# A GNN attention layer: leaky scores by absolute values, softmax sums once per chunk, and in the last chunk three of seven weight tiles made by ScalarE

## The chip, the cores and the metric

One core of one Trainium2 chip runs the whole program. The metric is the device time of one execution in microseconds (us); the kernel before took 5410.82 us (median of three runs, 5407.89 to 5411.46). The engines are TensorE (PE, with its weight loads as PEld), VectorE (DVE), ScalarE (ACT), GpSimd (POOL) and the DMA queues, most of which SyncE (SP) issues. Each engine works its own queue in order; they wait for one another by semaphores.

## The reference

A pre-norm graph attention layer on 12,500 nodes of 128 features and 412,500 edges of 64 features, cut to what matters:

```python
h = relu(layernorm(x))
q, k, v = h @ Wq + bq, h @ Wk + bk, h @ Wv + bv
attn_in = concatenate([q[src], k[tgt], edge @ We + be])
hmid   = leaky_relu(attn_in @ A1 + b1, 0.2)          # per edge, 128
scores = leaky_relu(hmid @ A2 + b2, 0.2)             # per edge, 8 heads
w      = softmax(scores.mean(heads), over all edges)
out    = segment_sum(w * v[tgt], src)
x + gamma * norm(h @ Wn + bn + out) + beta
```

A leaky value is linear in z and |z|: leaky(z) = 0.6 z + 0.4 |z| for a slope of 0.2. So the mean over eight heads is a sum of eight absolute values and one linear form, sum(z).

## The kernel before, in words

**Staging.** The edges are cut into four chunks (121, 109, 98 and 75 groups of 1024 edges). The first stage computes, for each tile of 128 edges, the k part of the hidden row and v (L809, L812), evicts them with ScalarE (L792, L795) and scatters each row by an indirect DMA of GpSimd (`scatter`, L747) into a table in HBM that is sorted into 98 blocks of 128 source nodes. The second stage reads each block back as 11, 10, 9 or 7 tiles of 128 slots (chunks 0 to 3) and does the rest. The first stage of chunk c+1 runs interleaved with the second stage of chunk c. The second stage of chunk 3, "the last chunk" below, has no first stage beside it. Then a final stage norms the nodes (L1193 to L1204).

**A block in the second stage**, with its jobs in `second_stage`: `load` brings the rows from HBM to `rows_of` (SP, L834; six buffers) and q for the block (L837). `places` turns the place column on PE (L841), `put_places` writes it out by ACT and a DMA (L846, L848), `spread_places` reads it back to all partitions (SP, L854), and `select` compares it on DVE (L861, `sel_q`). `turn` transposes four or three tiles on PE and adds q through `sel_q` (L870, L873) into `h_ps`; `steep` is the hidden leaky value, ACT (L881, `low`) and then DVE (L882). `heads_of` multiplies with A2 on PE (L889) into the one bank `s_ps`; `add_bias` evicts it with ACT (L896, `z`); `by_slot` is the scores' leaky value and a 32x32 transpose on DVE (L902, L904); `scores` masks and sums the heads on DVE (L910, L912, L916). `spread_top` transposes the row maxima on PE (L921), `greatest` keeps the running maximum on DVE (L930), `exponentials` makes exp and a fading factor on ACT (L938 or L941, L943), and `add_weights` adds to the sums on DVE (L948). `weights` makes one 128x128 matrix for each tile on DVE (L955: place equal to column, times the weight), `products` multiplies it with v on PE (L964, two passes for each tile), and `add_sums` adds the block into `acc` on DVE (L971, L973).

**What sets the order.** A plan written out by hand: `at(step, turn, job, block)` puts each job at a step, a step's jobs go by their turn, and each engine takes its instructions in exactly that order. A block of the last chunk has two quads (`nq` = 2; four tiles, then three) and takes four steps, so its plan repeats every four steps, with jobs of several blocks in each. `load` of a block may be issued when the products of the block six before it have been read.

The plan's repeating order before, in the last chunk, for one period:

```
PE:  places | products x3 | turn x3 | spread_top | products x4 | heads_of | turn x4
DVE: add_sums | weights x4 | greatest | steep x3 | select | weights x3 | add_weights | leaky | transpose | none | summed | score | steep x4
ACT: put_places | steep x3 | exp, fade | add_bias | steep x4
```

Of the kernel before, what the change touches and what calls it, by code (L numbers as in the profile page):

```python
# [10 lines left out]
FP = mybir.dt.float32  # L11
# [4 lines left out]
AF = mybir.ActivationFunctionType  # L16
ALU = mybir.AluOpType
AX = mybir.AxisListType
# [4 lines left out]
P = 128  # L23
D = 128
DE = 64
H = 8
EPS = 1e-5
SLOPE = 0.2
# [8 lines left out]
BUFS = 6  # L37

RROWS = 16

SPARE = 2

# [69 lines left out]
def kernel(ctx: ExitStack, tc: tile.TileContext, n_edges, x, src, dst, ea, w_nv, w_qt, w_kt,  # L112
# [12 lines left out]
    nc = tc.nc  # L125
    NP = x.shape[0]
    NTN = NP // P
# [8 lines left out]
    for i, share in enumerate(CHUNKS):  # L136
        n = NG - g0 if i == len(CHUNKS) - 1 else max(1, round(NG * share))
# [4 lines left out]
    NC = len(chunks)  # L142
    most_tiles = max(ct for _, _, ct, _ in chunks)

    blocks = []
# [24 lines left out]
    late = ctx.enter_context(tc.tile_pool(name="late", bufs=1))  # L170
# [16 lines left out]
    ones = const.tile([P, P], FP, name="ones")  # L187
# [23 lines left out]
    iota_f = iota("iota_f", P, 1, 1, 0)  # L211
# [15 lines left out]
    a2_sb = const.tile([P, 32], FP, name="a2_sb")  # L227
    nc.vector.memset(a2_sb, 0.0)
    nc.scalar.dma_start(out=a2_sb[:, :H], in_=a2)
    b2_col = const.tile([P, 1], FP, name="b2_col")  # L230
    nc.vector.memset(b2_col, 0.0)
    for g in range(4):
        nc.scalar.dma_start(out=b2_col[32 * g:32 * g + H, :], in_=b2.rearrange("a h -> h a"))
    nc.vector.tensor_scalar(a2_sb, a2_sb, 1.0 / H, None, op0=ALU.mult)
    nc.vector.tensor_scalar(b2_col, b2_col, 1.0 / H, None, op0=ALU.mult)


    w_ea = const.tile([P, 2, D], FP, name="w_ea")
    cp = ctx.enter_context(tc.tile_pool(name="count", bufs=2))
# [2 lines left out]
    ps_t = ctx.enter_context(tc.tile_pool(name="ps_t", bufs=1, space=PSUM))  # L242

    t_bank = ps_t.tile([P, 512], FP, name="t_bank")

    setup = ctx.enter_context(ExitStack())
    setup.enter_context(tc.manual_schedule(engines={ET.SP}))
# [397 lines left out]
    sums = late.tile([P, 1], FP, name="sums")  # L645

    less_of = [late.tile([P, NTN], FP, name=f"less_of{c}") for c in range(2)]
    nothing = late.tile([P, 1], FP, name="nothing")
    nc.vector.memset(nothing, 1e30)
    sums_of = late.tile([P, NTN], FP, name="sums_of")  # L650
    nc.vector.memset(sums_of, 0.0)

    def newest(top_of, old, new, pool):

# [169 lines left out]
    def second_stage():  # L824


        rows_of, qws, plss, state = {}, {}, {}, {}
# [70 lines left out]
        def by_slot(i):  # L898

            n = 32 * blocks[i][2]  # L900
            z = state["z"][:, 0:n]
            nc.vector.scalar_tensor_tensor(z, z, SLOPE, z, op0=ALU.mult, op1=ALU.max)  # L902
            state["zt"] = p3.tile([P, most_tiles * 32], FP, name="zt")
            nc.vector.transpose(state["zt"][:, 0:n], z)  # L904

        def scores(i):

            c, b, ct, _, _ = blocks[i]
            none = ps.tile([P, most_tiles], FP, name="none")[:, 0:ct]
            nc.vector.tensor_scalar(none, slot_of[c], filled[c % 3][:, b:b + 1], -1e30, op0=ALU.is_ge, op1=ALU.mult)  # L910
            summed = ps.tile([P, most_tiles], FP, name="summed")[:, 0:ct]
            nc.vector.tensor_reduce(summed, state["zt"][:, 0:32 * ct].rearrange("p (t h) -> p t h", h=32)[:, :, 0:H],  # L912
                                    AX.X, ALU.add)
            state["score", i] = score = ps.tile([P, most_tiles], FP, name="score")
            state["top"] = ps.tile([P, 1], FP, name="top_of")
            nc.vector.tensor_tensor_reduce(score[:, 0:ct], summed, none, 1.0, -3e38, op0=ALU.add, op1=ALU.max,  # L916
                                           accum_out=state["top"])
# [15 lines left out]
        def exponentials(i):  # L933
            c, b, ct, _, _ = blocks[i]
            score = state["score", i][:, 0:ct]
            less = less_of[c % 2][:, b:b + 1]
            if c == 0:
                nc.scalar.activation(score, score, AF.Exp, bias=less, accum_out=sums_of[:, b:b + 1])  # L938
            else:
                state["part", i] = ps.tile([P, 1], FP, name="part_of")  # L940
                nc.scalar.activation(score, score, AF.Exp, bias=less, accum_out=state["part", i])  # L941
                state["fade", i] = ps.tile([P, 1], FP, name="fade_of")
                nc.scalar.activation(state["fade", i], less_of[1 - c % 2][:, b:b + 1], AF.Exp, bias=less, scale=-1.0)  # L943

        def add_weights(i):
            c, b, _, _, _ = blocks[i]
            if c > 0:
                nc.vector.scalar_tensor_tensor(sums_of[:, b:b + 1], sums_of[:, b:b + 1], state["fade", i],  # L948
                                               state.pop(("part", i)), op0=ALU.mult, op1=ALU.add)

        def weights(i, q):
            state["w", i, q] = ws = []
            for t in range(q * QUAD, min((q + 1) * QUAD, blocks[i][2])):
                w = pw.tile([P, P], FP, name="w")
                nc.vector.tensor_scalar(w, iota_f, rows_of[i][:, t, 0:1], state["score", i][:, t:t + 1],  # L955
                                        op0=ALU.is_equal, op1=ALU.mult)
                ws.append(w)

        def products(i, q):
            ct = blocks[i][2]  # L960
# [17 lines left out]
        def at(when, turn_, job, *args):  # L978
            plan_of.setdefault(when, []).append((turn_, len(plan_of[when]) if when in plan_of else 0, job, args))

        for i, (c, b, ct, nq, i0) in enumerate(blocks):
            t = 2 * i0
            at(load_at(i), 2, load, i)
            first = t - 9 if nq > 2 else t - 8
            at(first, 3, places, i)
            at(first + 1, 0, put_places, i)
            at(first + 3, 0, spread_places, i)
            at(t - 1, 3, select, i)
            for q in range(nq):
                at(t + 2 * q, 1, turn, i, q)  # L990
                at(t + 2 * q + 1, 0, steep, i, q)
            t += 2 * nq
            at(t - 1, 3, heads_of, i)
            at(t, 0, add_bias, i)
            at(t + 1, -1, by_slot, i)
            at(t + 1, -1, scores, i)
            at(t + 2, 2, spread_top, i)
            at(t + 2, 3, greatest, i)
            at(t + 3, 2, exponentials, i)
            at(t + 4, 3, add_weights, i)  # L1000
            t = 2 * i0 + LAG
            for q in range(nq):
                at(t + 2 * q - 1, 0, weights, i, q)
                at(t + 2 * q, 1, products, i, q)
            at(t + 2 * nq - 1, 0, add_sums, i)
# [14 lines left out]
    def all_sums():  # L1020

        less = less_of[(NC - 1) % 2]
        most_of = late.tile([P, NTN], FP, name="most_of")
        nc.vector.tensor_scalar(most, less[:, NTN - 1:NTN], -1.0, None, op0=ALU.mult)
        nc.scalar.activation(most_of, less, AF.Exp, bias=less[:, NTN - 1:NTN], scale=-1.0)
        nc.vector.tensor_mul(sums_of, sums_of, most_of)
        nc.vector.tensor_reduce(sums, sums_of, AX.X, ALU.add)
        return most_of

    def count_left():  # L1030
# [4 lines left out]
    def other_edges(most_of):  # L1035

        with tc.tile_pool(name="others", bufs=1) as op, tc.tile_pool(name="others_ps", bufs=1, space=PSUM) as ops_:
            turns = nc.values_load(trips[0:1, NC:NC + 1], min_val=0, max_val=NG, skip_runtime_bounds_check_because=BECAUSE)
            with tc.For_i(0, turns, 1) as g:  # L1039
                b2_bc = op.tile([P, H], FP, name="b2_bc")  # L1040
                nc.sync.dma_start(out=b2_bc, in_=b2.to_broadcast([P, H]))
                nc.vector.tensor_scalar(b2_bc, b2_bc, 1.0 / H, None, op0=ALU.mult)
                ea_t = op.tile([P, halves * P], FP, name="ea_t")
                nc.sync.dma_start(out=ea_t, in_=ea.rearrange("g p f -> p g f")[:, ds(g, 1), :].rearrange("p a f -> p (a f)"))
                to = op.tile([P, SUPER], I32, name="to_n")
# [19 lines left out]
                z = op.tile([P, SUPER, H], FP, name="z_n")  # L1065
                v = op.tile([P, SUPER, D], FP, name="v_n")
                for k in range(SUPER):
# [28 lines left out]
                nc.vector.scalar_tensor_tensor(z, z, SLOPE, z, op0=ALU.mult, op1=ALU.max)  # L1096
                sc = op.tile([P, SUPER], FP, name="sc")
                nc.vector.tensor_reduce(sc, z, AX.X, ALU.add)
                none = op.tile([P, SUPER], FP, name="none_n")
                nc.vector.tensor_scalar(none, flag, 1e30, -1e30, op0=ALU.mult, op1=ALU.add)  # L1100
                nc.vector.tensor_add(sc, sc, none)
                fade, shift = newest(sc, most, most, op)
                nc.scalar.activation(sc, sc, AF.Exp, bias=shift, scale=1.0)
                part = op.tile([P, 1], FP, name="part_n")
# [6 lines left out]
                with tc.For_i(0, NTN, 1) as b:  # L1111
# [13 lines left out]
    for c in range(NC + 1):  # L1125
# [7 lines left out]
        if c > 0:  # L1133
            n = ends[c] - ends[c - 1]
# [7 lines left out]
        if c == 0:  # L1142
# [20 lines left out]
    with tc.tile_pool(name="last", bufs=1, reuse_waits="tile") as lp:  # L1163
# [12 lines left out]
        with tc.manual_schedule(engines={ET.SP, ET.Pool}):  # L1176
# [4 lines left out]
            part_of = all_sums()  # L1181
# [65 lines left out]
```

## Time and profile before

| | |
|---|---|
| median of three runs | 5410.82 us |
| the profiled execution | 5393.0 us; span on the core 5391.3 us |
| busy, share of span | PE 78%, PEld 55%, DVE 78%, ACT 40%, POOL 63% |
| first stage of chunk 0 and nodes, to 1466 us | PE 834, DVE 757, ACT 406, POOL 970 us busy of 1290 (from 176 us) |
| second stage of chunk 0, 1466 to 2676 us | PE 1056, DVE 1017, ACT 517, POOL 922 us busy of 1210 |
| of chunk 1, 2676 to 3781 us | PE 969, DVE 944, ACT 505, POOL 829 us busy of 1105 |
| of chunk 2, 3781 to 4687 us | PE 797, DVE 724, ACT 433, POOL 623 us busy of 906 |
| of chunk 3, 4724 to 5298 us | PE 458, DVE 517, ACT 225, POOL 8 us busy of 574 |
| final stage, 5298 us to the end | DVE 87 us busy of 94 |

The stages are read off the first and last instruction of the scatter (L747) and of `acc` (L971, L973). Engine times are busy times in that stretch and may lie beside each other. "Idle before" is the time an engine stood still ahead of an instruction, with what ended it.

### The profile page before, as it was taken

Reading aid. Unit: us, or ns where it says so; the run is one execution under the profiler, and the core shown is the slowest. Engines: PE = TensorE matmul, PEld = TensorE weight load, DVE = VectorE, ACT = ScalarE, POOL = GpSimd, SP = SyncE. Lnnn points to the kernel's source line nnn. Section 1 sums busy time; section 2 is a strip of 40 time slices with the busy share of each in tenths; the row PEclk is TensorE's granted clock in tenths of the full one; section 3 lists DMA queues with packets and bytes.
Section 4 is the critical chain, followed back from the end, with each engine's and each line's share of the span. In section 5 each row is a group of like instructions: output and inputs, shape, how many; then the busy total and the mean of one; then the engine's idle time right before and its main releaser. Section 6 shows DMA issues by size and latency. Waiting matters only on the chain. (4 is left out here: it accounts for less than half of the span.)

```text
span 5391.3 us, 90152 instructions
## 1 busy us (share of the span) xinstructions
PE 4218.1 (78%) x26817; PEld 2951.6 (55%) x27160; DVE 4204.3 (78%) x13299; ACT 2160.8 (40%) x6046; POOL 3379.1 (63%) x3261
## 2 busy tenths in 40 slices
PE   4777766565588888998788888987888888878782
PEld 2344433333266666666566666665666666655551
DVE  7777754544378888888788988887877788799889
ACT  1344422222244444444344444443444444434333
POOL 0477777777677777777667777777666666500002
PEclk8788887777789999999999999999999999999996
DMA  8677765555489999888789999988899998755554
GB/s 244 201 234 228 230 196 162 169 164 167 162 262 290 280 280 282 279 281 281 251 257 284 289 284 282 282 286 260 263 284 280 276 287 284 242 194 193 190 194 164
DMA packets 609678, 1309.97 MB, mean 243 GB/s; under 512 B 117392, under 2 KB 371524, under 8 KB 571168
## 3 DMA queue, kind: packets, MB, share of 16 engines
q1 hardware_dynamic: 404312, 841.81, 53.1%
q0 software_dynamic: 154704, 424.26, 21.8%
q10 hardware_dynamic: 50168, 38.07, 2.2%
q8 instruction: 218, 3.57, 0.3%
q14 instruction: 276, 2.26, 0.1%
HBM read 782.14 MB, written 521.60 MB: 242 GB/s over the span
## 5 line engine op out<-in xcount | busy, mean ns | idle before, releaser
L747 POOL DMA_INDIRECT tab<-row,slots x3223 | 3343.9, 1038 | 1339.5 <-issue 702.8
L809 PE MATMUL row_ps<-w_ea,ea_t 128*128 128x256 f32 x3224 | 1105.0, 427 | 379.2 <-ACT row L795 311.5
L964 PE MATMUL o_ps<-rows_of,w 128*128 128x128 f32 x7252 | 1073.6, 287 | 127.9 <-DVE w L955 125.7
L964 PEld LDWEIGHTS o_ps<-rows_of,w 128*128 128x128 f32 x7252 | 954.8, 193 | 254.7 <-DVE w L955 199.7
L795 ACT ACTIVATE row<-row_ps 128x512 f32<-128x512 f32 x1612 | 939.6, 590 | 279.7 <-PE row_ps L812 215.7
L955 DVE TENSOR_SCALAR w<-iota_f,rows_of,score 128x128 f32<-128x128 f32 x3626 | 1037.2, 356 | 0.8 <-ACT score L938 0.8
L809 PEld LDWEIGHTS row_ps<-w_ea,ea_t 128*128 128x128 f32 x3224 | 577.9, 208 | 680.9 <-ACT row L795 397.7
L881 ACT ACTIVATE low<-h_ps 128x512 f32<-128x512 f32 (+3 forms) x1078 | 569.0, 528 | 848.7 <-PE h_ps L873 690.8
L873 PE MATMUL h_ps<-sel_q,qw 128*128 128x512 bf16 (+3 forms) x2891 | 753.7, 344 | 60.1 <-DVE sel_q L861 40.2
L882 DVE TENSOR_TENSOR rows_of<-h_ps,low 128x512 f32<-128x512 f32 (+3 forms) x1078 | 648.2, 601 | 134.7 <-ACT low L881 121.3
L812 PE MATMUL row_ps<-kv,sel 126*128 126x256 bf16 x3224 | 666.3, 290 | 1.5 <-DVE sel L785 1.5
L792 ACT ACTIVATE row<-place 128x4 f32<-128x4 bf16 x806 | 166.9, 207 | 1219.5 <-DMA tab<-row,slots 1195.7
L870 PE MATMUL h_ps<-ident,rows_of 128*128 128x128 f32 x3626 | 592.9, 279 | 0.0
L450 DVE TENSOR_TENSOR one<-bins_b,block 128x500 f16<-128x500 bf16 x646 | 301.5, 467 | 326.8 <-PE run L457 322.8
L812 PEld LDWEIGHTS <-sel 126*128 126x128 bf16 x3224 | 337.6, 105 | 279.3 <-issue 55.0
L870 PEld LDWEIGHTS h_ps<-ident,rows_of 128*128 128x128 f32 x3626 | 433.1, 143 | 102.2 <-issue 39.5
L503 DVE TENSOR_REDUCE num<-run 128x5 f32<-128x500 f32 x646 | 433.4, 671 | 11.8 <-PE run L457 11.8
L861 DVE TENSOR_SCALAR sel_q<-pls,part 128x1408 bf16<-128x1408 uint8 (+3 forms) x392 | 330.6, 843 | 108.5 <-DMA pls<-pl_d 108.0
L1174 POOL TENSOR_TENSOR xt<-xt,affine 128x640 f32<-128x640 f32 (+1 forms) x20 | 32.7, 1649 | 608.2 <-DMA xt<-in_x 595.4
L873 PEld LDWEIGHTS <-qw 128*128 128x128 bf16 x3234 | 314.9, 99 | 160.7 <-issue 54.6
L889 PE MATMUL s_ps<-rows_of,a_sb 128*32 128x352 f32 (+3 forms) x3136 | 292.2, 444 | 117.2 <-DVE rows_of L882 116.1
L457 PE MATMUL run<-one,rest_b 128*128 128x500 f16 x642 | 268.9, 419 | 145.1 <-DVE num L503 143.9
(195 smaller groups left out, 4161.9 us busy)
## 6 DMA issues: line engine op xcount, KB each, us to landing
rows_of<-tab SPq DMA_DIRECT2D x98, 1413.5 KB
rows_of<-tab SPq DMA_DIRECT2D x98, 1285.0 KB
rows_of<-tab SPq DMA_DIRECT2D x98, 1156.5 KB
ea_t<-in_ea SPq DMA_DIRECT2D x403, 256.0 KB
rows_of<-tab SPq DMA_DIRECT2D x98, 899.5 KB
tab<-row,slots POOLq DMA_INDIRECT x3223
offs<-off_d SPq DMA_DIRECT2D x403, 126.0 KB
tab<-blank SPq DMA_DIRECT2D x196, 257.0 KB
```

Source lines behind the costliest of these rows:

```text
L503: nc.vector.tensor_reduce(num, strips[:, :, :m].rearrange("p b m -> p m b"), AX.X, ALU.max)
L747: i = nc.gpsimd.indirect_dma_start(out=tabs[c % 2][:, :], out_offset=bass.IndirectOffsetOnAxis(ap=slots[c][t // (8 * STR)][:m, t % (8 * ST ...
L795: nc.scalar.activation(row[:, :, 1:ROW], bank, AF.Copy)
L809: nc.tensor.matmul(bank[:, :, 0:D], lhsT=ea_g[:, ts(k, P)], rhs=w_ea, start=True, stop=False, skip_group_check=True)
L812: nc.tensor.matmul(bank[:, b, :], lhsT=sel[:, ts(b * halves + k, P)], rhs=kv, start=False, stop=True, skip_group_check=True)
L861: nc.vector.tensor_scalar(sel[:, 0:n], plss[i][:, 0:n], part1, None, op0=ALU.is_equal)
L870: nc.tensor.matmul(h_ps[:, ts(j, P)], lhsT=rows_of[i][:, q * QUAD + j, 1:D + 1], rhs=ident, is_transpose=True, start=j == 0, stop=False, s ...
L873: nc.tensor.matmul(h_ps[:, 0:m * P], lhsT=qws[i][:, ts(k, D)], rhs=plss[i][:, q * QUAD * P:(q * QUAD + m) * P], start=False, stop=k == 2, ...
L881: nc.scalar.activation(low, h_ps, AF.Copy, scale=SLOPE)
L882: nc.vector.tensor_max(rows_of[i][:, q * QUAD:q * QUAD + m, 1:D + 1], h_ps.rearrange("p (j e) -> p j e", j=m), low.rearrange("p (j e) -> p ...
L955: nc.vector.tensor_scalar(w, iota_f, rows_of[i][:, t, 0:1], state["score", i][:, t:t + 1], op0=ALU.is_equal, op1=ALU.mult)
L964: nc.tensor.matmul(state["o_ps"][:, 0:D], lhsT=w, rhs=rows_of[i][:, t, D + 1:ROW], start=t == 0, stop=t == ct - 1)
```

## The change

Six edits.

1. A2 and b2 are scaled by 0.4/8 instead of 1/8, and a ninth column holds 1.5 times the sum of the eight. `by_slot` loses its leaky instruction; `scores` sums eight absolute values and adds the ninth column to the mask by a new `tensor_add`.
2. b2 is laid out as a row and turned into a column by a matmul at the start.
3. `sums_of` becomes two tiles, one for even and one for odd chunks. `exponentials` writes each block's sum into its own column, and `sum_chunk` folds a chunk's 98 columns into `sums` once per chunk.
4. `add_weights` is therefore planned once per chunk, not per block.
5. In the last chunk tiles 1, 3 and 5 of a block get their weight matrix from two ScalarE instructions: Abs(place - column), then Relu(weight - 4 times that).
6. In the last chunk `heads_of` goes one step later, and with it all that follows from it up to the exponentials. `weights` and `products` keep their steps.

```diff
-            z = state["z"][:, 0:n]
-            nc.vector.scalar_tensor_tensor(z, z, SLOPE, z, op0=ALU.mult, op1=ALU.max)
-            nc.vector.transpose(state["zt"][:, 0:n], z)
+            nc.vector.transpose(state["zt"][:, 0:n], state["z"][:, 0:n])
...
-            nc.vector.tensor_reduce(summed, state["zt"][:, 0:32 * ct].rearrange("p (t h) -> p t h", h=32)[:, :, 0:H],
-                                    AX.X, ALU.add)
+            zt = state["zt"][:, 0:32 * ct].rearrange("p (t h) -> p t h", h=32)
+            nc.vector.tensor_reduce(summed, zt[:, :, 0:H], AX.X, ALU.add, apply_absolute_value=True)
+            nc.vector.tensor_add(none, none, zt[:, :, H])
...
-            if c == 0:
-                nc.scalar.activation(score, score, AF.Exp, bias=less, accum_out=sums_of[:, b:b + 1])
-            else:
-                state["part", i] = ps.tile([P, 1], FP, name="part_of")
-                nc.scalar.activation(score, score, AF.Exp, bias=less, accum_out=state["part", i])
+            nc.scalar.activation(score, score, AF.Exp, bias=less, accum_out=sums_of[c % 2][:, b:b + 1])
+            if c > 0:
                 state["fade", i] = ps.tile([P, 1], FP, name="fade_of")
...
-        def add_weights(i):
-            c, b, _, _, _ = blocks[i]
-            if c > 0:
-                nc.vector.scalar_tensor_tensor(sums_of[:, b:b + 1], sums_of[:, b:b + 1], state["fade", i],
-                                               state.pop(("part", i)), op0=ALU.mult, op1=ALU.add)
+        def add_weights(c):
+            sum_chunk(c, p3.tile([P, NTN], FP, name="most_in"))
...
                 w = pw.tile([P, P], FP, name="w")
+                ws.append(w)
+                if blocks[i][0] == NC - 1 and t in PEAKS:
+                    nc.scalar.activation(w, iota_f, AF.Abs, bias=rows_of[i][:, t, 0:1], scale=-1.0)
+                    nc.scalar.activation(w, w, AF.Relu, bias=state["score", i][:, t:t + 1], scale=-4.0)
+                    continue
                 nc.vector.tensor_scalar(w, iota_f, rows_of[i][:, t, 0:1], state["score", i][:, t:t + 1],
                                         op0=ALU.is_equal, op1=ALU.mult)
...
-            at(t - 1, 3, heads_of, i)
+            if nq > 2:
+                at(t - 1, 3, heads_of, i)
+            else:
+                at(t, 2, heads_of, i)
+                t += 1
             at(t, 0, add_bias, i)
...
-            at(t + 4, 3, add_weights, i)
+            if b == NTN - 1 and c < NC - 1:
+                at(t + 4, 4, add_weights, c)
```

`PEAKS` is (1, 3, 5). `sum_chunk`, new:

```python
def sum_chunk(c, most_in):
    less = less_of[c % 2]
    nc.scalar.activation(most_in, less, AF.Exp, bias=less[:, NTN - 1:NTN], scale=-1.0)
    if c > 0:
        fade = late.tile([P, 1], FP, name="fade_sums")
        nc.scalar.activation(fade, less_of[1 - c % 2][:, NTN - 1:NTN], AF.Exp, bias=less[:, NTN - 1:NTN], scale=-1.0)
    nc.vector.tensor_mul(sums_of[c % 2], sums_of[c % 2], most_in)
    part = late.tile([P, 1], FP, name="part_sums")
    nc.vector.tensor_reduce(part if c > 0 else sums, sums_of[c % 2], AX.X, ALU.add)
    if c > 0:
        nc.vector.scalar_tensor_tensor(sums, sums, fade, part, op0=ALU.mult, op1=ALU.add)
```

The built program's repeating order in the last chunk, after:

```
PE:  places | products x3 | turn x3 | products x4 | spread_top | turn x4 | heads_of
DVE: steep x4 | transpose | none | summed | add | score | add_sums | weights 0, 2 | steep x3 | greatest | select | weights 4, 6
ACT: add_bias | steep x4 | put_places | weights 1, 3 | steep x3 | weight 5 | exp, fade
```

More of the change, by code (lines that the diff above doesn't have):

```diff
@@ L39 @@
 RROWS = 16
+PEAKS = (1, 3, 5)
 SPARE = 2
@@ L230 @@
     b2_col = const.tile([P, 1], FP, name="b2_col")
[L231 to L235, printed above, removed]
+    bend, line = (1.0 - SLOPE) / 2.0, (1.0 + SLOPE) / (1.0 - SLOPE)
+    nc.vector.tensor_scalar(a2_sb, a2_sb, bend / H, None, op0=ALU.mult)
+    nc.vector.tensor_reduce(a2_sb[:, H:H + 1], a2_sb[:, 0:H], AX.X, ALU.add)
+    nc.vector.tensor_scalar(a2_sb[:, H:H + 1], a2_sb[:, H:H + 1], line, None, op0=ALU.mult)
     w_ea = const.tile([P, 2, D], FP, name="w_ea")
@@ L244 @@
     t_bank = ps_t.tile([P, 512], FP, name="t_bank")
+    with tc.tile_pool(name="bias_row", bufs=1) as bp:
+        b2_row = bp.tile([1, 4, 32], FP, name="b2_row")
+        nc.vector.memset(b2_row, 0.0)
+        for g in range(4):
+            nc.scalar.dma_start(out=b2_row[:, g, 0:H], in_=b2)
+        nc.vector.tensor_scalar(b2_row, b2_row, bend / H, None, op0=ALU.mult)
+        nc.vector.tensor_reduce(b2_row[:, :, H], b2_row[:, :, 0:H], AX.X, ALU.add)
+        nc.vector.tensor_scalar(b2_row[:, :, H], b2_row[:, :, H], line, None, op0=ALU.mult)
+        nc.tensor.matmul(t_bank[:, 0:1], lhsT=b2_row.rearrange("p g h -> p (g h)"), rhs=ones[0:1, 0:1], start=True, stop=True)
+        nc.vector.tensor_copy(b2_col, t_bank[:, 0:1])
     setup = ctx.enter_context(ExitStack())
@@ L649 @@
     nc.vector.memset(nothing, 1e30)
-    sums_of = late.tile([P, NTN], FP, name="sums_of")
-    nc.vector.memset(sums_of, 0.0)
+    sums_of = [late.tile([P, NTN], FP, name=f"sums_of{c}") for c in range(2)]
+    def sum_chunk(c, most_in):
[7 more added lines that the diff above has]
+        nc.vector.tensor_reduce(part if c > 0 else sums, sums_of[c % 2], AX.X, ALU.add)
+        if c > 0:
+            nc.vector.scalar_tensor_tensor(sums, sums, fade, part, op0=ALU.mult, op1=ALU.add)
     def newest(top_of, old, new, pool):
@@ L936, in exponentials @@
             less = less_of[c % 2][:, b:b + 1]
-            if c == 0:
-                nc.scalar.activation(score, score, AF.Exp, bias=less, accum_out=sums_of[:, b:b + 1])
-            else:
-                state["part", i] = ps.tile([P, 1], FP, name="part_of")
-                nc.scalar.activation(score, score, AF.Exp, bias=less, accum_out=state["part", i])
+            nc.scalar.activation(score, score, AF.Exp, bias=less, accum_out=sums_of[c % 2][:, b:b + 1])
+            if c > 0:
                 state["fade", i] = ps.tile([P, 1], FP, name="fade_of")
                 nc.scalar.activation(state["fade", i], less_of[1 - c % 2][:, b:b + 1], AF.Exp, bias=less, scale=-1.0)
-        def add_weights(i):
-            c, b, _, _, _ = blocks[i]
-            if c > 0:
-                nc.vector.scalar_tensor_tensor(sums_of[:, b:b + 1], sums_of[:, b:b + 1], state["fade", i],
-                                               state.pop(("part", i)), op0=ALU.mult, op1=ALU.add)
+        def add_weights(c):
+            sum_chunk(c, p3.tile([P, NTN], FP, name="most_in"))
         def weights(i, q):
@@ L954, in weights @@
                 w = pw.tile([P, P], FP, name="w")
+                ws.append(w)
[3 more added lines that the diff above has]
+                    continue
                 nc.vector.tensor_scalar(w, iota_f, rows_of[i][:, t, 0:1], state["score", i][:, t:t + 1],
                                         op0=ALU.is_equal, op1=ALU.mult)
-                ws.append(w)
         def products(i, q):
@@ L1024, in all_sums @@
         nc.vector.tensor_scalar(most, less[:, NTN - 1:NTN], -1.0, None, op0=ALU.mult)
-        nc.scalar.activation(most_of, less, AF.Exp, bias=less[:, NTN - 1:NTN], scale=-1.0)
-        nc.vector.tensor_mul(sums_of, sums_of, most_of)
-        nc.vector.tensor_reduce(sums, sums_of, AX.X, ALU.add)
+        sum_chunk(NC - 1, most_of)
         return most_of
@@ L1041, in other_edges @@
                 nc.sync.dma_start(out=b2_bc, in_=b2.to_broadcast([P, H]))
-                nc.vector.tensor_scalar(b2_bc, b2_bc, 1.0 / H, None, op0=ALU.mult)
+                nc.vector.tensor_scalar(b2_bc, b2_bc, bend / H, None, op0=ALU.mult)
                 ea_t = op.tile([P, halves * P], FP, name="ea_t")
@@ L1098, in other_edges @@
                 nc.vector.tensor_reduce(sc, z, AX.X, ALU.add)
+                nc.vector.tensor_scalar(sc, sc, 1.0 / bend, None, op0=ALU.mult)
                 none = op.tile([P, SUPER], FP, name="none_n")
```

## The prediction

> **What bounds the kernel now.** I read the engines' busy time by stage, then the waits of each stage, then the timeline of one block. The stretches are the second stages of chunks 0, 1, 2 (each with a first stage beside it) and of the last chunk alone.
>
> ```profile
> 1466.00:2676.00 1210.00, 1055.69 (x7045) 765.89 (x7139) 1016.55 (x3122) 516.55 (x1321) 921.54 (x872) 0.96 0.88 277
> 3781.00:4687.00 906.00, 796.78 (x5658) 592.12 (x5757) 724.35 (x2356) 432.89 (x1239) 622.91 (x599) 0.99 0.90 278
> 4724.00:5298.00 574.00, 457.63 (x3484) 328.61 (x3529) 517.04 (x1920) 225.01 (x665) 7.88 (x5) 0.98 0.57 190
> ```
>
> The columns are length, then PE, PEld, DVE, ACT, POOL busy, the clock, the DMA share and GB/s. In the mixed stages (3221 us) PE, DVE, POOL and DMA are all between 69% and 90%. In the last chunk DVE stands at 517 of 574 us, 90%, and looks like the bound. The waits say otherwise:
>
> ```profile
> PE t_bank L841 <- DMA rows_of<-tab: 56.5, 50, 3.4
> DVE acc L973 <- PE o_ps L964: 46.7, 84, 3.3
> ```
>
> In 84 of 98 blocks DVE stands idle ahead of `acc`, because PE had stood at `places` until the rows landed. One block's timeline shows the loop:
>
> ```profile
> 4908.27 0.33 SPq L834 DMA_DIRECT2D rows_of<-tab  x1
> ...
> 4913.21 0.27 PE L841 MATMUL t_bank<-ident,rows_of 128*7 128x128 f32 x1 [0.49 <-DMA rows_of<-tab]
> 4913.31 0.83 PE L964 MATMUL o_ps<-rows_of,w 128*128 128x128 f32 x6
> 4914.18 0.33 SPq L834 DMA_DIRECT2D rows_of<-tab  x1
> 4914.19 0.35 DVE L973 SCALAR_TENSOR_TENSOR acc<-acc,fade_of,o_ps 128x128 f32<-128x128 f32 x1
> 4914.45 1.11 DVE L955 TENSOR_SCALAR w<-iota_f,rows_of,score 128x128 f32<-128x128 f32 x4
> 4914.80 0.27 PE L921 MATMUL s_ps<-ident,top_of 128*128 128x128 f32 x1
> 4914.91 1.20 PE L964 MATMUL o_ps<-rows_of,w 128*128 128x128 f32 x8
> 4915.48 0.35 DVE L930 TENSOR_SCALAR_CACHE_REDUCE s_ps<-s_ps,less_of 128x128 f32<-128x128 f32 x1
> 4916.22 0.68 DVE L861 TENSOR_SCALAR sel_q<-pls,part 128x896 bf16<-128x896 uint8 x1
> 4916.36 0.60 PE L889 MATMUL s_ps<-rows_of,a_sb 128*32 128x224 f32 x8 [0.25 <-DVE rows_of L882]
> 4917.02 0.45 ACT L896 ACTIVATE z<-s_ps,b_col 128x224 f32<-128x224 f32 x1 [0.52 <-PE s_ps L889]
> 4917.38 0.81 PE L873 MATMUL h_ps<-sel_q,qw 128*128 128x512 bf16 x3
> 4918.13 0.41 DVE L904 STREAM_TRANSPOSE zt<-z 128x224 f32<-128x224 f32 x1
> 4918.23 0.60 ACT L881 ACTIVATE low<-h_ps 128x512 f32<-128x512 f32 x1 [0.76 <-PE h_ps L873]
> 4918.91 0.69 DVE L882 TENSOR_TENSOR rows_of<-h_ps,low 128x512 f32<-128x512 f32 x1
> ```
>
> A load issued at 4908.27 lets `places` start at 4913.21; the three products behind it free the buffer that the next load (4914.18) waits for. That is 4.94 + 0.97 us here; over the 98 loads the median from issue to `places` is 4.78, so 5.75 in all, which is also the median interval between two updates of `acc` (mean 5.92, as some loads take 2 us more). So **the last chunk runs at the pace of one load in flight at a time**. DVE's own queue needs about 5.3 (5.75 less its typical idle 0.5), little less.
>
> **The change, part by part.**
>
> *DVE in the mixed stages.* The leaky instruction goes: L902 took 0.52, 0.49 and 0.45 us for 11, 10 and 9 tiles. `add_weights` goes where it was (chunks 1, 2; L948, 0.22). The new `tensor_add` on 128x7 to 128x11 has no row; the nearest are L916 (0.17) and L912 (0.21 to 0.27), and I take 0.2. Net for a block 0.32, 0.51 and 0.47 us, for 98 blocks each 31 + 50 + 46 = 127 us of DVE time. It is worth 127 us if DVE ended everything last, and nothing if another resource covers it. What covers it:
>
> ```profile
> ACT row L792 <- DMA tab<-row,slots: 508.4, 226, 7.2
> PE o_ps L964 <- DVE w L955: 116.9, 138, 3.7
> PE s_ps L889 <- DVE rows_of L882: 91.7, 77, 4.2
> DVE sel_q L861 <- DMA pls<-pl_d: 90.1, 72, 2.6
> ```
>
> (1500 to 4600 us.) For 508 us ACT is ahead, waiting until GpSimd's scatters have read the row ring; GpSimd has 76% busy and 17% issue in chunk 0's stage. PE waits for DVE 209 us in all, and in chunk 2's stage DVE waits for the places' DMA. So only about 209 of 3100 us, 7%, are stretches where a faster DVE is what PE needs, with every gain capped there by POOL, DMA (0.88 to 0.90) and PE (87%). I take 25 us, a fifth of 127, nearer to nothing; the ends 0 and 127 stay for the range.
>
> *DVE and ACT in the last chunk.* DVE loses three weights (L955, 0.26 apart), the leaky 0.39 and `add_weights` 0.13, and gains the add: its queue falls from 5.3 to about 4.2 us a block. ACT gains six instructions. None of that form is in the trace; a 128x128 ACTIVATE without a tensor bias took 0.274 (L881's small form), and the bias of `z` costs 0.09 (0.447 against 0.355 on L881's line between 128 and 512 columns), so 0.37 each, 2.2 us. ACT's own 2.6 us become 4.8 a block, within the period; weights 1 and 3 come after `put_places` and have until the second and fourth product. If that cover is gone, each late pair costs PE up to 0.8 us.
>
> *The order in the last chunk.* This is the part that decides. Before, `heads_of` stood ahead of `turn x4` on PE, so that ACT evicted `z` while PE turned, and `spread_top` stood ahead of `products x4`. After, each engine's queue (front of the document) makes one closed chain, which must be run through once per block. Followed from `heads_of`, with the timeline's durations and start-to-start distances; 0.05 is what lies between the end on one engine and the start on the next (4916.96 to 4917.02):
>
> - `heads_of` 0.60, to ACT 0.05;
> - `add_bias` 0.35 (0.45, the next overlaps it by 0.1), and only then `low` of `steep x4`, 0.60 + 0.05, since it stands behind it in ACT's queue;
> - on DVE `steep x4` 0.61, transpose 0.34, mask 0.11, sum 0.24, add 0.15, score 0.09, `add_sums` 0.26, weight 0 0.34 + 0.05. All of this now stands ahead of the weights, as `z` comes late;
> - on PE `products x4` 1.08, `spread_top` 0.27 + 0.05, now behind the products;
> - on DVE `greatest` 0.27, and behind it `select` 0.68 + 0.05, which `turn x4` needs;
> - on PE the three L873 of `turn x4` 0.70 to the start of `heads_of`.
>
> Sum: 0.65 + 0.35 + 0.65 + 1.80 + 0.39 + 1.08 + 0.32 + 0.27 + 0.73 + 0.70 = **6.94 us a block**. The load loop needs 5.75, so the load is no longer late; the chain is. The same kind of sum for before is about 4.6 (`heads_of`, `z`, leaky to score, `steep x4`, `add_sums`, four weights, `greatest`, `steep x3`), under the load's 5.75, which is why it was not seen. Each term is bound by how well neighbours overlap; half an overlap less or more on most links gives 6.6 to 7.3.
>
> Cost: 97 blocks x (6.94 - 5.92) = 99 us. Loads that take more than the chain still show: ten intervals of before lie above 6.94, by 7 us in all. So +106 us, between +70 and +140.
>
> *The rest.* The b2 row adds four small DVE operations of 0.2 and one round trip to PE ahead of the first casts (10.36 us in the trace), about 1 us. `sum_chunk` is some 1 us three times inside idle stretches of ACT, and at the end replaces nearly the same instructions. Together +1 us.
>
> **A page weighed.** The last chunk's row says DVE 90% busy. The Trainium skill, Perfetto Trace Analysis, section Identifying the Most-Contended Engine, says to optimize the engine with the highest occupancy first, and its section Optimizing Scalar/DVE Operations says that offloading to ScalarE may make sense when DVE is saturated. By that reading the last chunk should gain; the trace disagrees so far, since DVE is idle ahead of `acc` in 84 of 98 blocks. It is rival B below.
>
> **The rivals.**
>
> A. *The load keeps the pace.* If the chain does not close, for instance because `z` is evicted earlier than I think, the last chunk stays at one load per 5.75 us and only the mixed stages gain: 5411 - 25 = 5386, faster. It decides wherever the chain is shorter than 5.75, that is 1.2 us less than I add up. For it: the load loop is untouched and sure. Against it: every link is either data or the order within one queue.
>
> B. *DVE was the bound.* The last chunk falls with DVE's queue, by 5.3 - 4.2 = 1.1 us for 98 blocks, 108 us, and 25 before: 5278. Against it are the 46.7 us of DVE's waits and the unchanged load.
>
> C. *The mixed stages give back everything.* DVE's 127 us come off in full: -127 + 106 = -20, so 5391. For it: PE's waits for DVE, 209 us. Against it: 508 us of ACT waiting for the scatters.
>
> D. *ACT becomes the bound.* A switch of tables between Abs and Exp would cost 1.283 us each (the trace's ACT_TABLE_LOAD), two a block, 2.6 us on top of ACT's 4.8 and right in the chain: 98 x 2.6 = 251 us more, about 5744. Against it: Relu (L574) ran beside Sqrt and Square, and Copy and Identity beside Exp, with four loads in the whole trace. The Trainium skill, ScalarE: Activation LUTs, section Table sets, has abs and relu in every set, by which D is out; Abs itself no run here shows.
>
> **How the numbers follow.** Forecast: +106 - 25 + 1 = +82 us. On the profiled execution's own 5393 that gives 5475; the median of the runs lies 18 above it, so 5411 + 82 = **5493**. Chances: forecast 0.82, A 0.07, B 0.04, C 0.04, D 0.03. The forecast's own ends are +70 with 55 gained before (5426) and +140 with nothing gained (5552); larger gains run into C. The range 5415 to 5555 leaves out A, B, D and C. What a measurement of this kernel can tell from no change is about 0.2%, 11 us. Faster: A, B and half of C, 0.13; same 0.03; slower 0.84.
>
> **What would show it.** The step of the last chunk is right if the median interval of `acc` goes from 5.75 to about 6.9, PE no longer waits at `places` for the DMA, and instead waits in `products x4` for weight 0 and in `turn x4` for `sel_q`, with DVE waiting for `low` and for `spread_top`. It is wrong if `places` still waits for `rows_of`. The mixed stages are right if the three stretches together lose 0 to 55 us of 3221 with DVE's busy time down by about 127. A load of ACT's table in every block would show D.

## The result, and the profile after

| | before | changed |
|---|---|---|
| median, same chip (4 runs each) | 5409.35 us (5401.93 to 5411.46) | 5484.32 us (5481.94 to 5491.33) |
| the profiled execution | 5393.0 us, span 5391.3 | 5484.8 us, span 5483.0 |
| start and first stage of chunk 0 | 1466.1 | 1474.0 |
| second stages of chunks 0, 1, 2 | 1210.2, 1104.7, 905.7 | 1207.1, 1099.9, 911.9 |
| gap from the last scatter to the first `acc` of the last chunk | 37.0 | 39.8 |
| last chunk | 574.1 | 655.2 |
| final stage | 93.6 | 95.1 |
| interval between two `acc` of the last chunk: median, mean | 5.75, 5.92 | 6.80, 6.75 |

The changed kernel takes 1.0143 times as long, interval 1.0126 to 1.0161. The forecast was 5493 in a range from 5415 to 5555. Of the 91.7 us between the two profiled spans, 81.1 lie in the last chunk; the three mixed stages differ by -1.7 together. The profiled execution of before is 16 us under that kernel's median, the changed kernel's is at its own, so differences of that size between stages of these two profiles carry little weight.

The stretches of the changed kernel (length, then PE, PEld, DVE, ACT, POOL busy, clock, DMA share, GB/s) for chunk 0, chunk 2 and the last chunk:

```profile
1474.00:2681.00 1207.00, 1063.28 (x7141) 771.03 (x7140) 978.54 (x3123) 518.05 (x1321) 912.41 (x872) 0.95 0.89 278
3781.00:4693.00 912.00, 804.99 (x5764) 597.39 (x5762) 670.86 (x2258) 433.60 (x1238) 616.40 (x599) 0.98 0.89 276
4733.00:5388.00 655.00, 456.43 (x3528) 307.70 (x3528) 416.20 (x1535) 403.27 (x1245) 8.09 (x5) 0.99 0.52 166
```

DVE's busy time in the last chunk has fallen from 517 to 416 us and ACT's has risen from 225 to 403, as the edits say, and no engine is over 70% busy. Yet the stretch is longer, at the same clock (0.99, 0.98 before). An engine table alone can't say why; the waits of that stretch can:

```profile
DVE rows_of L906 <- ACT low L905: 178.4, 95, 1.9
PE o_ps L985 <- DVE w L977: 141.8, 99, 2.7
ACT z L920 <- PE s_ps L913: 131.2, 94, 2.4
DVE s_ps L953 <- PE s_ps L944: 43.7, 96, 1.1
```

Four waits, each about once per block, join ACT, DVE and PE into a ring. PE's wait for the rows at `places` (L865), 56.5 us before, is no longer in the list, and the idle time ahead of `acc` has fallen from 46.7 to 2.2 us. One block's timeline shows the ring (start, duration, engine, line; the brackets are idle time and what ended it):

```profile
5001.61 0.60 PE L913 MATMUL s_ps<-rows_of,a_sb 128*32 128x224 f32 x8
5002.27 0.45 ACT L920 ACTIVATE z<-s_ps,b_col 128x224 f32<-128x224 f32 x1 [1.39 <-PE s_ps L913]
5002.62 0.59 ACT L905 ACTIVATE low<-h_ps 128x512 f32<-128x512 f32 x1
5003.24 0.69 DVE L906 TENSOR_TENSOR rows_of<-h_ps,low 128x512 f32<-128x512 f32 x1 [1.91 <-ACT low L905]
5003.85 0.40 DVE L926 STREAM_TRANSPOSE zt<-z 128x224 f32<-128x224 f32 x1
...
5004.42 0.16 DVE L936 TENSOR_TENSOR none<-none,zt 128x7 f32<-128x7 f32 x1
...
5004.70 0.34 DVE L994 SCALAR_TENSOR_TENSOR acc<-acc,fade_of,o_ps 128x128 f32<-128x128 f32 x1
...
5004.96 0.59 DVE L977 TENSOR_SCALAR w<-iota_f,rows_of,score 128x128 f32<-128x128 f32 x2
...
5005.35 1.16 PE L985 MATMUL o_ps<-rows_of,w 128*128 128x128 f32 x8 [1.45 <-DVE w L977]
...
5006.35 0.27 PE L944 MATMUL s_ps<-ident,top_of 128*128 128x128 f32 x1
...
5006.66 0.36 DVE L953 TENSOR_SCALAR_CACHE_REDUCE s_ps<-s_ps,less_of 128x128 f32<-128x128 f32 x1 [0.44 <-PE s_ps L944]
...
5006.94 0.68 DVE L885 TENSOR_SCALAR sel_q<-pls,part 128x896 bf16<-128x896 uint8 x1
...
5007.67 0.81 PE L897 MATMUL h_ps<-sel_q,qw 128*128 128x512 bf16 x3 [0.61 <-DMA qw<-q_tab]
...
5008.41 0.60 PE L913 MATMUL s_ps<-rows_of,a_sb 128*32 128x224 f32 x8
```

Read from bracket to bracket: each wait ends within 0.1 us of the end, on the engine named, of what it waits for. The last bracket names the DMA of q, but `sel_q` ends at 5007.62 and PE starts at 5007.67, so it is `sel_q`. From `heads_of` at 5001.61 to the next at 5008.41 are **6.80 us**; the forecast added up 6.94. The 10th and the 90th percentile of the interval are 6.80 too: nearly every block goes at the ring's pace.

### The profile page after: what moved, and what is told of

The parts are those of the page before. It is cut to its first block, busy times and chain, and to the rows that moved or that the text cites. A ratio compares the mean times of both kernels' runs of the same rounds, so it can differ in the third digit from the quotient of the medians.

```text
span 5483.0 us, 90244 instructions
## 1 busy us (share of the span) xinstructions
PE 4232.5 (77%) x27162; PEld 2941.5 (54%) x27162; DVE 3957.6 (72%) x12724; ACT 2339.6 (43%) x6640; POOL 3367.0 (61%) x3261
## 5 line engine op out<-in xcount | busy, mean ns | idle before, releaser
L977 DVE TENSOR_SCALAR w<-iota_f,rows_of,score 128x128 f32<-128x128 f32 x3332 | 957.5, 352 | 0.9 <-ACT score L960 0.9
L897 PE MATMUL h_ps<-sel_q,qw 128*128 128x512 bf16 (+3 forms) x3234 | 779.1, 350 | 105.1 <-DVE sel_q L885 54.8
L897 PEld LDWEIGHTS <-qw 128*128 128x128 bf16 x3234 | 315.1, 99 | 241.3 <-issue 137.0
L920 ACT ACTIVATE z<-s_ps,b_col 128x352 f32<-128x352 f32 (+3 forms) x392 | 198.4, 506 | 453.1 <-PE s_ps L913 452.7
```

What stands on the lines that cost most here:

```text
L897: nc.tensor.matmul(h_ps[:, 0:m * P], lhsT=qws[i][:, ts(k, D)], rhs=plss[i][:, q * QUAD * P:(q * QUAD + m) * P], start=False, stop=k == 2, ...
```

## The experiments

Ratios are to the kernel before on the same chip; its medians there were 5366 to 5389 us, so times of different chips are not set beside one another. "Interval" is that between two `acc` of the last chunk. The theory: edit 6 closes the ring, and edits 1 to 5 are worth little. The rivals: ScalarE's weights are in the ring, or what was gained in the mixed stages was eaten elsewhere.

### Edit 6 undone

```diff
-            if nq > 2:
-                at(t - 1, 3, heads_of, i)
-            else:
-                at(t, 2, heads_of, i)
-                t += 1
+            at(t - 1, 3, heads_of, i)
```

> The changed kernel with edit 6 undone: heads_of stands ahead of turn x4 again, and z and the scores with it; ScalarE still makes weights 1, 3 and 5. Theory (the closed chain through the late heads_of set 6.80 us a block): the chain opens, the last chunk falls back to one load in flight, a median interval of acc of about 5.75 us and a mean of about 5.9, so 97 x (6.75 - 5.9) = 80 us less than the changed kernel, about 5405 us. Rival (ScalarE's six new instructions, 0.4 us each, slow the last chunk): the interval stays near 6.8 and the time near 5484. Rival (it is both): in between, 5430 to 5460.

Ratio 0.9963 [0.9947, 0.9979], interval 5.67 (mean 5.83), last chunk 565.3 us. The ring is gone, and the wait that the forecast named for before is back, in the waits of the last chunk:

```profile
PE t_bank L865 <- DMA rows_of<-tab: 41.6, 87, 3.0
```

So edit 6 alone turns a small gain into the loss. This version is 0.4% faster than the kernel before, and faster than the changed one.

### Edit 6 alone

The same five lines, put into the kernel before.

> The kernel before with edit 6 alone: heads_of one step later, all weights on VectorE, leaky and add_weights as before. Theory (closed chain): the chain of the changed kernel, 6.80, loses the add (0.19 and 0.13 to the sum instead of 0.24: 0.08 less) and gains leaky (0.42) and add_weights (0.13) between steep x4 and add_sums: about 7.3 us a block, 97 x (7.3 - 5.92) = 134 us over the kernel before, about 5540. Rival (ScalarE's weights were the cause): without them the last chunk stays at 5.75 and the time at 5409.

Ratio 1.0330 [1.0306, 1.0354], interval 7.38 (mean 7.54), last chunk 731.7 us. Edit 6 suffices, and costs more without the others. Its size came out 0.1 above the expected 7.3.

### ScalarE's weights back on VectorE, edit 6 kept

```diff
-PEAKS = (1, 3, 5)
+PEAKS = ()
```

> The changed kernel with edit 5 undone: VectorE makes all seven weights, heads_of is late as in the changed kernel. Theory (closed chain): the weights that moved to ScalarE were not on the chain, since weight 0 comes first either way and VectorE has 6.8 us for a queue of about 4.9; interval 6.8, time about 5484 as the changed kernel. Rival (ScalarE's weights delay PE's products): the interval falls, towards 5.75, and the time by up to 80 us.

Ratio 1.0168 [1.0148, 1.0189], interval 6.90, last chunk 665.7 us. Without them the ring is 0.1 longer, not shorter; they don't cause the loss. Beside the 7.38 of edit 6 alone, edits 1 to 4 take 0.48 out of the ring, where the leaky instruction and the block's sum less the new add come to 0.37 (0.39 + 0.13 - 0.15).

### Edits 1 to 4 alone

Edit 6 undone and `PEAKS = ()`.

> Edits 1 to 4 alone: absolute values, ninth column, sums once per chunk; heads_of early, all weights on VectorE. The chunks before the last have the same instructions as in the changed kernel. Theory: the last chunk is back at the load's 5.75 (mean 5.9), and VectorE's relief of about 127 us in the earlier stages is hidden beside the scatters, PE and the DMAs, as the changed kernel's stage lengths say (3.1 and 4.8 us less, 6.2 us more): 5400 to 5412. Rival (the relief counts and the changed kernel lost it elsewhere): 25 us or more under the kernel before, 5385 or less. Rival (the absolute sums cost time themselves): over 5420.

Ratio 0.9977 [0.9967, 0.9987], -12 us; interval 5.72, last chunk 566.2 us. The mixed stages take 3208.5 us here, 3209.9 and 3200.4 in the two other runs with edits 1 to 4 on this chip, and 3220.8 with edit 6 alone, which leaves these stages as before: 11 to 20 us less. The runs below give the same on two other chips: 3183 to 3190 us in three with edits 1 to 4 beside 3197 without, and 3204 and 3201 beside 3218. The changed kernel's own 1.7 us is the exception, and is taken from a profile of before that is 16 us under its median. With and without ScalarE's weights (the first experiment and this one) the last chunk takes 565.3 and 566.2 us and the intervals of the ratios overlap, so no gain from three weights on ScalarE is shown.

### One link of the ring taken out: the row maxima ahead of the products

```diff
-            at(t + 2, 2, spread_top, i)
+            at(t + 2, 2 if nq > 2 else 0, spread_top, i)
```

> The changed kernel, heads_of late, but in the last chunk spread_top is planned ahead of products x4 on PE instead of behind them. Theory (closed chain): products x4 and the way back from them leave the chain; what is left goes over VectorE from add_sums: heads_of to add_sums 3.61 us as measured (0.66 + 0.35 + 0.62 + 0.61 + 0.33 + 0.11 + 0.13 + 0.19 + 0.09, and 0.52 for the ends), then weights 0 and 2, steep x3, greatest, select and the three L897: about 6.1 us a block instead of 6.80, so 97 x 0.7 = 65 us under the changed kernel, about 5420 beside 5484. If the chain is right but the link through spread_top is not on it, the interval stays 6.80.

Ratio 1.0042 [1.0027, 1.0056], interval 6.26, with both percentiles at 6.26 or 6.27. DVE's wait for `spread_top`, 43.7 us in the changed kernel, is no longer among its waits: the products have left the ring, and 0.54 us go, of the 0.7 expected.

### Another: z behind the hidden rows

```diff
-            at(t, 0, add_bias, i)
+            at(t, 0 if nq > 2 else 1, add_bias, i)
```

> The changed kernel, heads_of late, but in the last chunk ScalarE evicts z behind low and put_places, not ahead of them. Theory (closed chain): low no longer waits for heads_of, which takes 0.7 us out of the chain (z 0.35 and part of low and steep x4 now run beside heads_of and places): about 6.1 us a block, about 65 us under the changed kernel. If VectorE's steep x4 and low are not on the chain: 6.8 or more, as z itself comes later by 0.9.

Ratio 1.0097 [1.0062, 1.0132], interval 6.51: 0.3 us gained, of 0.7 expected. The timeline shows why (heads_of at 5000.23):

```profile
5001.08 0.27 ACT L870 ACTIVATE plT<-t_bank 7x128 uint8<-7x128 f32 x1
...
5001.69 0.45 ACT L920 ACTIVATE z<-s_ps,b_col 128x224 f32<-128x224 f32 x1 [0.34 <-ACT plT L870]
...
5002.17 0.41 DVE L926 STREAM_TRANSPOSE zt<-z 128x224 f32<-128x224 f32 x1 [0.51 <-ACT z L920]
```

ACT now does `low`, `put_places` with the start of its DMA, and only then `z`, 1.46 us after `heads_of` instead of 0.66. The ring leaves `low` out but goes through `z` instead, and DVE waits 0.51 for it. `put_places` in its turn waits for `places`, which PE does behind `heads_of` (its end, 5001.04, is 0.04 ahead of L870). The expectation had left out this detour.

### Can the load's pace be beaten? Places later

If one load in flight at a time is the pace of before, `places` a step later should free the next load's buffer sooner. In the kernel before, and in the first experiment's:

```diff
-            first = t - 9 if nq > 2 else t - 8
+            first = t - 9 if nq > 2 else t - 7
```

> The kernel before, with places planned one step later in the last chunk, so that PE takes products x3 (which free a buffer) ahead of places: the next load is issued before the one under way has landed. Theory on the kernel before (one load in flight sets 5.75): now VectorE's queue of about 5.3 sets the pace, places no longer waits for rows_of; 97 x (5.9 - 5.35) = 53 us under the kernel before, ratio about 0.990. Rival (VectorE was the bound of the last chunk all along, as its 90% say): no change within 0.2%.

> The changed kernel with edit 6 undone (heads_of early) and places one step later in the last chunk, as in the run on the kernel before. With the load out of the way, ScalarE's weights should pay at last: VectorE's queue is 4.2 us, PE's 4.5, and a chain over ScalarE (weights 1 and 3, put_places, low, then VectorE, heads_of, turn x4) some 5.25. Theory: 5.0 to 5.3 us a block, about 60 us under the kernel before with the 12 us of edits 1 to 4, ratio 0.985 to 0.990. Rival (the DMAs cannot deliver a block faster than about 5.7): ratio 0.996 as with edit 6 undone alone.

Ratios 1.0037 [1.0025, 1.0049] and 1.0073 [1.0045, 1.0101]: both missed. In the first, the fastest tenth of the intervals falls to 5.32, but the slowest rises to 7.50 and the mean is 6.06. The waits of its last chunk have a new one, where the compare of the places waits for their DMA:

```profile
DVE sel_q L861 <- DMA pls<-pl_d: 59.7, 43, 2.6
```

`places` later makes the places late, so these two don't test the load alone.

### Can it be beaten? More buffers

The six buffers of eleven tiles hold nine blocks of seven. As a ring, the last chunk may have more loads in flight; its load is planned two steps earlier and waits for the block nine before.

```diff
+            if "ring" not in state:
+                state["ring"] = pb.tile([P, BUFS * most_tiles, ROW], FP, name="rows_of")
+            first = i % BUFS * most_tiles if c < NC - 1 else b % (BUFS * most_tiles // ct) * ct
+            rows_of[i] = state["ring"][:, first:first + ct, :]
...
-        t = 2 * i0 - (17 if nq > 2 else 11)
+        t = 2 * i0 - (17 if nq > 2 else 13)
```

Put into the kernel before, into the first experiment's, and into edits 1 to 4 alone:

> The kernel before, with the memory of the six row buffers used as one ring: in the last chunk, where a block has 7 tiles and not 11, it holds nine blocks, and a load is issued two steps earlier, behind the places' DMA, without waiting for PE. All engines keep their order. The run with places one step later did not settle what bounds the kernel before, as it made a new wait for the places' DMA. Theory (one load in flight sets 5.75): places no longer waits for rows_of and the median interval falls to VectorE's queue, about 5.33 us, with fewer long ones; 97 x (5.92 - 5.4) = 50 us under the kernel before, ratio about 0.991. Rival (the interval is VectorE's chain anyway): 5.75 stays, ratio 1.000.

> The changed kernel with edit 6 undone, and nine buffers in the last chunk as in the run beside it. VectorE's queue is 4.2 us a block and PE's 4.5, but ScalarE's weights stand in a chain of their own (weights 1 and 3, 1.4 us, put_places, low, steep x3, heads_of, turn x4, low): about 5.25 us. Theory: 5.2 to 5.4 us a block, ratio 0.985 to 0.989 with the 0.2% of edits 1 to 4; faster than both kernels. Rival (the DMAs cannot deliver more often): 5.7, ratio 0.996.

> Edits 1 to 4 with nine buffers in the last chunk, all weights on VectorE. VectorE's queue is then 5.33 - 0.42 - 0.13 + 0.2 = 4.95 us; with z, low and steep x4 not quite hidden some 5.2 to 5.3. Theory: within 0.2% of the run beside it with ScalarE's weights, that is moving three weights to ScalarE brings nothing even with the load out of the way, because a chain and not VectorE's queue then sets the pace. Rival (VectorE's queue sets it): ScalarE's weights gain 0.7 us x 97 = 70 us, 1.3%.

Ratios 1.0054 [1.0033, 1.0074], 1.0029 [1.0016, 1.0043] and 1.0021 [1.0010, 1.0033]; mean intervals 6.16, 6.13 and 6.18. All three missed, and the last two don't differ beyond their intervals. In the kernel before with the nine buffers, a load takes 6.26 us from issue to its last packet (4.28 before), 4.99 from first to last packet (3.31 before), and the places come late as well: `sel_q` waits 50.6 us for their DMA.

But this is not the price of more loads in flight, for there were hardly more: only 11 of 97 loads have a packet under way when the next load's first one starts. SyncE's queue, too, is in order, and the plan puts the load right behind the places' DMA (`pls`), which waits until `put_places` has written the places:

```profile
5005.99 0.32 SPq L857 DMA_DIRECT2D pls<-pl_d  x1
5006.36 0.43 SPq L837 DMA_DIRECT2D rows_of<-tab  x1
...
5011.87 0.32 SPq L857 DMA_DIRECT2D pls<-pl_d  x1
5012.24 0.42 SPq L837 DMA_DIRECT2D rows_of<-tab  x1
```

SyncE stands at `pls` for 371 us of the 490 from 4760 to 5250, and 94 of 98 loads are issued within 0.6 us of it. That closes another ring, over two blocks. Its medians are 6.26 from a load's issue to its last packet, 1.12 on to the issue of that write, 4.47 on to that of `pls` (1.27 before) and 0.37 on to the load two blocks later: 12.22, or 6.11 a block, beside a measured mean of 6.16. So these runs don't test what more loads in flight would bring, nor, with the pace set by that ring, what ScalarE's weights would.

What stretched the loads is not settled. The row packets of 7196 B still take 337 ns each, those of 896 B that carry the places 116 instead of 48 ns on average, and the DMA engines are 64% busy (58% before). The long loads are those beside the places: 93 of the 98 have 32 or more of the 896 B packets between their first and last packet, the other five take 3.4 us. In the changed kernel 92 loads have none and take 3.2 us, and the four with 32 or more take 5.0.

### VectorE made slower in the mixed stages

One more leaky instruction for each block of chunks 0 to 2, in the kernel before; its result is overwritten.

```diff
             state["zt"] = p3.tile([P, most_tiles * 32], FP, name="zt")
+            if blocks[i][0] < NC - 1:
+                nc.vector.scalar_tensor_tensor(state["zt"][:, 0:n], z, SLOPE, z, op0=ALU.mult, op1=ALU.max)
```

> The kernel before with the scores' leaky instruction issued a second time in the chunks before the last, into a tile that the transpose overwrites at once: 294 more VectorE instructions of 0.45 to 0.52 us, 0.42 apart at least, some 135 us of VectorE time in 3221 us, about as much as edits 1 and 4 take away there. Theory (VectorE is covered by the scatters, PE and the DMAs there): 5 to 25 us more, as the other sign gave about 12. Rival (VectorE ends last): 135 us more, 2.5%.

Ratio 1.0041 [1.0024, 1.0058], +22 us (13 to 31); DVE is busy 127 us longer in these stages than in the profile of before. So a microsecond of VectorE's time there costs 0.10 to 0.25 when added, and is worth 0.05 to 0.14 when taken away (7 to 20 us of the mixed stages for 141). The ranges overlap, so no difference between the two directions is shown.

## Why the prediction was right, point by point

- **The ring decides: right, and shown** by the timeline, by edit 6 undone and alone, and by two links taken out, each of which shortens the ring. Its links, in the forecast's order, against what was added up:

| | predicted | measured |
|---|---|---|
| `heads_of` to `z` | 0.65 | 0.66 |
| `z` to `low` | 0.35 | 0.35 |
| `low` to `steep x4` | 0.65 | 0.62 |
| `steep x4` through `add_sums` | 1.80 | 1.72 |
| weight 0 to products | 0.39 | 0.39 |
| products to `spread_top` | 1.08 | 1.00 |
| `spread_top` to `greatest` | 0.32 | 0.31 |
| `greatest` to `select` | 0.27 | 0.28 |
| `select` to PE | 0.73 | 0.73 |
| L897 to the next `heads_of` | 0.70 | 0.74 |
| sum | 6.94 | 6.80 |

- **The last chunk's term was mis-sized**: +106 forecast, +81 measured. 97 x 0.14 = 14 of it is the ring's own length (the products' and DVE's neighbours overlap more than the rows of before showed), and 7 is the allowance for long loads. Those no longer show at all: the 90th percentile of a load's first to last packet has fallen from 4.72 to 3.43 us, beside a loop that starts one every 6.80. The rest, 4 us, is that the mean interval is 6.75 and not 6.80, 97 x 0.05.
- **The mixed stages' term was mis-sized**: -25 forecast, -1.7 in the profiled execution, but -7 to -20 in the eight other runs with edits 1 to 4, each beside a run without them on its chip, and -13 on average. That DVE's relief is mostly covered was right; DVE's busy time fell by 141 us (127 forecast), and the longest of the waits that the forecast named as covering it is there as before (1500 to 4600 us):

```profile
ACT row L816 <- DMA tab<-row,slots: 541.9, 219, 8.1
```

- PE's wait for the weights is 112.7 us beside 116.9, and ACT's for the scatters has risen to 541.9 us from 508.4. The fifth that I took was too much; a tenth is what the runs bear. The two errors in the sum, 25 too much in the last chunk and 12 to 23 too little in the mixed stages, nearly cancel, so part of the closeness of 5484 to 5493 is luck.
- **The rest**: +1 forecast. Outside the stages of the table's middle the profiled execution has +2.0 at the start, +5.8 in chunk 0's first stage, +2.8 in the gap and +1.5 at the end. The first and the last fit the b2 row and the new sum; the 5.8 are not shown to come from the edits, since that stage takes 1288.6 to 1294.5 us (1290.4 before) in the eight other profiles that have edits 1 to 4 and do the same work there; what they are no run tells.
- **Rivals.** A (the load keeps the pace) is out, since no wait at `places` is left. B (DVE was the bound) is out: with edit 6 undone DVE falls to 434 of 565 us in the last chunk, and the interval only to 5.67. The Trainium skill, Perfetto Trace Analysis, section Identifying the Most-Contended Engine, would start with the engine of the highest occupancy; here that engine, 90% busy, was relieved of 83 us in the last chunk by edits 1 to 5, and the stretch fell by 9; relieved of 101 by all six, it grew by 81. C is out by the stages. D is out by the lines of ACT in the last chunk:

```profile
L975 ACT ACTIVATE w<-w,score 128x128 f32<-128x128 f32 x290 | 116.4, 402 | 9.4
L974 ACT ACTIVATE w<-iota_f,rows_of 128x128 f32<-128x128 f32 x289 | 113.2, 392 | 31.7 <-ACT plT L870 31.7
```

- Abs and Relu took 0.39 and 0.40 us (0.37 estimated), and the trace has four ACT_TABLE_LOADs, as before, none in the last chunk. The Trainium skill, ScalarE: Activation LUTs, section Table sets, has both functions in every set; the trace agrees.
- **The reading of before: right as far as its waits go, otherwise open.** SyncE's own waits show it as well (4640 to 5290 us):

```profile
SPq L834 <- PE o_ps L964: 389.0, 93, 6.6
```

- The next load waits for the products, which stand on PE behind `places`, which waits for the load under way. DVE's own queue of 5.3 us shows as the fastest tenth (5.32) once `places` is later. The forecast's "about 4.6" for the chain of before is too low: with the distances of the same block it comes to 0.66 + 0.50 + 1.20 + 0.74 + 0.26 + 1.03 + 0.27 + 0.61 = 5.27, still under 5.75. Whether the last chunk would go faster with more loads in flight, as this reading suggests, is untested, since the runs that were to show it made a ring through SyncE instead. That the places' packets are what stretches a load is suggested by which loads are long, not shown.

## What to carry to other kernels

Where an order is written out by hand, add up the closed chain of one period across the in-order queues, with start-to-start distances from a timeline: it gave 6.94 for 6.80 here, while the busy shares pointed the other way. Putting one instruction later on its queue moves all that waits for its result behind what already stands in the other queues; here five moved lines cost about 1.8% and undoing them made the rest of the change a gain of 0.4%. Price a relief of a busy engine by what else waits in that stage; 141 us of VectorE's time were worth about 12. And the queue that issues the DMAs is one of the in-order queues: before a run is taken as a test of more loads in flight, its timeline has to show two of them at once.

## What the runs showed of the hardware

- A load of 900 KB took 3.2 us from first to last packet with none of the places' 896 B packets in between (92 loads of the changed kernel), and about 5.0 with 32 or more of them (93 loads of the kernel before with nine buffers), while a row packet took 333 to 337 ns in both. Their number alone doesn't decide: in the kernel before 44 loads with 32 to 95 of them took 3.4.
- The write of the places, 0.9 KB, held up what waits for it when it was issued behind a load: from its issue to that of the DMA that waits for it the median is 1.27 us in the kernel before, where the next load is issued 0.4 after the write, but 3.45 in the changed kernel, where the load is issued 0.2 ahead of it, and 4.47 with nine buffers, 1.0 ahead.
- Long loads were no fixed cost to be added: the 90th percentile from first to last packet was 4.72 us in the kernel before, 4.04 in the run with VectorE made slower, whose last chunk is the same, 3.73 with edit 6 undone and 3.43 in the changed kernel.
